# A mixture-of-experts kernel: the last, small groups gathered earlier, and turned inside the first groups of later kinds

## The chip, the cores and the metric

The kernel runs on one core of a Trainium2 chip. The metric is the time of one execution on the device in microseconds (us); several executions are measured and their median is given. The engines are PE (matrix products), DVE (vector), ACT (activation functions), POOL (GpSimd, which here also issues the DMAs with a list of rows) and SP (issues the other DMAs). Each engine runs its own list of instructions in order and waits for the others by semaphores.

## The reference

The input is x of 4 x 1024 tokens of 256 channels. There are two layers, each wrapped as x + layernorm(layer(layernorm(x))). The first is a recurrence over the 1024 steps with a gate; the second is attention with 16 heads followed by four experts, of which each token uses two:

```python
px = einsum('btc,dc->btd', x, W_state) + b_state
g = sigmoid(einsum('btc,dc->btd', x, W_gate) + b_gate)
state = tanh(p_t + state)                  # step by step; out is g_t * state
...
x = x + ao                                 # causal attention, channels 0..63 of ao zeroed
xf = _rms(x, n2_w).reshape(-1, C)
probs = softmax(xf @ gate_w.T)
topv, topi = top_k(probs, 2)               # weights wts, two of four not zero
o0 = gelu(xf @ e0_up.T) @ e0_down.T
o1 = silu(xf @ e1_w1.T) * (xf @ e1_w2.T) @ e1_down.T
o2 = gelu(gelu(gelu(xf @ e2_l1.T) @ e2_l2.T) @ e2_l3.T) @ e2_l4.T
o3 = gelu(gelu(xf @ e3_down.T) @ e3_up.T) @ e3_out.T
moe = wts[:, 0:1]*o0 + wts[:, 1:2]*o1 + wts[:, 2:3]*o2 + wts[:, 3:4]*o3
```

## The kernel before

**Stages.** Up to about 1040 us the kernel computes the recurrence and, beside it, the attention. It writes one row per token into the DRAM tensor `row_d`: 256 channels after attention, 256 of the residual, four expert weights and the factor of the RMS norm (517 numbers). The experts follow, and the change is there.

**Kinds, groups, tails.** The gate sorts the tokens by the pair of experts that they use: six pairs, the *kinds*. Their order of work is `order = [3, 0, 1, 2, 4, 5]`; the place in this order is called the *turn number* n here. So n=0 is the pair (1, 2), n=1 is (0, 1), n=2 (0, 2), n=3 (0, 3), n=4 (1, 3) and n=5 (2, 3). How many tokens a kind has is known only when the kernel runs. A kind is worked off in groups of 256 tokens. Its first group always runs. Each further one stands inside an If (line 1728) on the count and runs if more than 128 tokens are left. What is left then, 1 to 128 tokens, is the kind's *tail*: six Ifs at the very end (line 1742), one for each kind in the same order, each with one group of 128 rows inside. An engine passes each If with a branch of its own; PE gets a hint where its branch will lead. Where an If is not entered, each engine runs a small other block, in which it raises its semaphores to the values that the skipped block would have left. On POOL this includes an instruction that raises the semaphore of a skipped DMA.

**What a group needs.** `fetch` (line 1516) gathers the rows of a group by their numbers, one DMA of 128 rows per half, issued by POOL, into a buffer: `rwfirst` for first groups, `rwsecond` for second ones, `rwnext` for the others, `rwtail` for tails, which have one buffer for each kind. `turn` makes the transposed input: DVE scales the rows (line 1531) into a buffer `x`, PE transposes it into PSUM (line 1538), ACT copies it to SBUF (line 1544). First groups and tails share one buffer `x`, the other groups have another. All turns share one PSUM bank (`tbanks`), which is free again when ACT has copied. `group` runs the products: the layers of the two experts (line 1561 on PE; activations on ACT, line 1622, or for expert 1 a tanh on ACT, line 1629, and DVE, lines 1632 and 1638), the last layer of each (line 1581), and adds their outputs to the rows (line 1649, DVE). Then the layer norm: statistics on DVE (lines 1662 and 1663), z and r on POOL (1669 and 1670), the rest on DVE (1675 and 1678), and a DMA by POOL that writes the rows to `out` (line 1681). Hidden layers pass through three PSUM banks in tails and later groups, two in first groups.

**What sets the order.** A planner written by hand, `plan.run`. Every piece of work is a generator that yields operations with an estimated cost, a priority and the events that it reads; the planner always issues the one that could start first by its own estimate, by priority where several could. What it issues becomes the fixed order of each engine's list. It plans one group at a time: all operations of a call of `group`, those of the list `then` among them, come before the branch that follows.

**Where fetches and turns stand.** A first group of turn n carries in `then`: the gather of its own third group, those of the first and second group of turn n+2, the gather of the tail of turn n−1 (for the last turn also that of its own tail), the turn of the first group of turn n+1, and the turn of its own second group. The first group of n=0 has a list of its own. A tail's turn stands in the tail itself.

Of the kernel before, what the change touches and what calls it, by code (L numbers as in the profile page):

```python
# [31 lines left out]
KINDS = E * (E - 1) // 2  # L32
# [146 lines left out]
class Plan:  # L179
# [14 lines left out]
    def ev(self, *key):  # L194
        return self.events.setdefault(key, Ready())
# [13 lines left out]
    def done(self, *key):  # L209
        self.ev(*key).at = self.end  # L210

    def give(self, *what):

        for w in what:
            if isinstance(w, int):
                self.banks.free[w] = self.end + self.HOP
            else:
                w[0].free[w[1]] = self.end + self.HOP
# [35 lines left out]
def sandwich(  # L254
# [1099 lines left out]
    def gate(pr, w, sm):  # L1354
# [36 lines left out]
    ])  # L1391
    inner.close()
    experts(
        tc, plan, banks, av, ident, mhalf, route, weights, keys, values, row_d, out,
        [after([NT - 1]), experts_input([NI - 1])],
# [4 lines left out]
def experts(  # L1400
# [69 lines left out]
    order = [EARLY] + [c for c in range(KINDS) if c != EARLY]  # L1470
    turn_of = {c: n for n, c in enumerate(order)}

    def kind(n):
        return order[n] if n < KINDS else None


    TAIL = "tail"
    x_tail = slots(KINDS, [P, NCC, P], "xtail").tiles

    def of(c, g):  # L1480
        if g == TAIL:
            return "next", turn_of[c]
        return ("first", turn_of[c] % 2) if g == 0 else ("next", g % 2)

    def xT_of(c, g):
        what, k = of(c, g)
        return x_tail[k] if g == TAIL else xTs[what][k]

    def tiles_of(g):
        return 1 if g == TAIL else NT2  # L1490

    def rows_of(c, g):
        if (c, g) == (EARLY, 0):
            return route["early_rows"]
        n = turn_of[c]
        if g == TAIL:
            return rows["tail"][n]
        what, k = ("first", n) if g == 0 else ("second", n) if g == 1 else ("next", g)
        return rows[what][k % 3]

    def ids_of(c, g, t):
        if (c, g) == (EARLY, 0):
            return route["early"][:, t : t + 1]
        if g == TAIL:
            return route["tails"][:, c : c + 1]
        at = (c * TOKENS + g * N) // P + t
        return ids[:, at : at + 1]

    def fetch(c, g, at=0.0):

        if c is None or g != TAIL and g * N >= TOKENS:
            return
        rw = rows_of(c, g)
        for t in range(tiles_of(g)):
            yield Op("POOL", 1.25, at, [ev("tails" if g == TAIL else "ids")], lag=3.0)
            nc.gpsimd.indirect_dma_start(
                out=rw[:, t, :], out_offset=None, in_=row_d[:, :],
                in_offset=bass.IndirectOffsetOnAxis(ap=ids_of(c, g, t), axis=0),
            )
            done("rows", c, g, t)  # L1520

    def turn(c, g):

        what, k = of(c, g)
        nt = tiles_of(g)
        rw, x = rows_of(c, g), xs["first" if g == TAIL else what][0]
        for t in range(nt):
            got = yield Op("DVE", 0.36, 3.0, [ev("rows", c, g, t)], [] if t else [tbanks["any"]])
            if got:
                tb, = got  # L1530
            nc.vector.tensor_scalar(
                x[:, t, :], rw[:, t, 0:C], rw[:, t, ROW - 1 : ROW], None, ALU.mult
            )
            done("xs", c, g, t)
        yield Op("PE", 0.6, 5.0, [ev("xs", c, g, t) for t in range(nt)], lag=0.2)
        for cc in range(NCC):
            for t in range(nt):
                nc.tensor.transpose(  # L1538
                    tb[0].tiles[tb[1]][:, cc, t * P : (t + 1) * P],
                    x[:, t, cc * P : (cc + 1) * P], ident,  # L1540
                )
        done("xT0", c, g)
        yield Op("ACT", 0.62, 0.5, [ev("xT0", c, g)])
        nc.scalar.copy(xT_of(c, g), tb[0].tiles[tb[1]][:, :, : nt * P])
        give(tb)
        done("xT", c, g)
# [148 lines left out]
    def groups(c, g):  # L1695

        n = turn_of[c]
        more = (g + 1) * N < TOKENS
        label = f"kind{c}group{g + 1}"
        if more and n_of:  # L1700
            hint(label, c, (g + 1) * N + P)
        then = [fetch(c, g + 2)]
        if g == 0:
            then += [fetch(kind(n + 2), 0), fetch(kind(n + 2), 1)]
            for before in [order[n - 1]] if n else []:
                then.append(fetch(before, TAIL, 1.0))
            if n + 1 == KINDS:
                then.append(fetch(c, TAIL, 1.0))
            else:
                then.append(turn(kind(n + 1), 0))  # L1710
        if more:
            then.append(turn(c, g + 1))
        if (c, g) == (EARLY, 0):
            then = [
                *gates, turn(c, 0), fetch(c, 1, 0.0), fetch(kind(1), 0, 1.0), fetch(c, 2, 2.0),
                fetch(kind(1), 1, 3.0), fetch(kind(2), 0, 4.0), fetch(kind(2), 1, 5.0),
                turn(c, 1), turn(kind(1), 0),
            ]
        group(c, g, then)
        if not n_of:  # L1720
            n_of.extend(
                nc.values_load_multi_w_load_instructions(
                    route["counts"][0:1, :], min_val=0, max_val=TOKENS,
                    skip_runtime_bounds_check_because="counts of tokens, only compared",
                )[1]
            )
        if more:
            with tc.If(  # L1728
                n_of[c] > (g + 1) * N + P, preferred_fallthrough_block=True, label=label
            ):  # L1730
                groups(c, g + 1)

    def hint(label, c, at):

        tc.mark_branch_hint_location(label, n_of[c] > at, engines=[mybir.EngineType.PE])

    n_of = []
    for c in order:
        groups(c, 0)
    for n, c in enumerate(order):  # L1740
        hint(f"tail{n}", KINDS + c, 0)
        with tc.If(n_of[KINDS + c] > 0, preferred_fallthrough_block=True, label=f"tail{n}"):
            group(c, TAIL, [turn(c, TAIL)])


# [57 lines left out]
```

## Time and profile before

| | |
|---|---|
| median of 9 runs | 1474.71 us |
| lowest, highest | 1470.46, 1477.03 us |
| the profiled execution | 1471.84 us |
| its span, from first to last instruction | 1470.1 us |
| PE busy | 1311.8 us (89% of the span) |
| DVE, ACT, POOL busy | 896.8, 705.8, 465.6 us |
| mean granted clock of PE | 0.947 of full speed |

The page's row of clocks and its row of PE in 40 slices of the span (36.8 us each, tenths) show where PE is not busy or not at full speed:

```profile
PE   4578787998999998999999999999899999999964
...
PEclk8799899999998989998999999999999999999987
```

Sixteen groups of 256 and two tails run in this execution, by the writes to `out` in the trace: 2 halves of n=0's first group, 10 of the other first groups, 8 of second groups, 12 of later ones, and 2 tails. A wait in the timeline stands in brackets after the instruction that waited: how long its engine was idle before it, and what ended that. A small q after an engine (POOLq) means its queue of instructions: branches, semaphores and the issuing of DMAs, which are not counted as busy. DMA issues by POOL are shown with the time that it takes to issue them, not with that of the transfer.

### The profile page before, as it was taken

The page shows a single profiled execution, that of the slowest core. Times are in us where ns is not written, and L with a number is a line of the kernel's source. Part 1 is how long each engine was busy: PE and PEld are TensorE (multiplying, and loading weights), DVE is VectorE, ACT ScalarE, POOL GpSimd, SP SyncE. Part 2 cuts the span into 40 slices and gives each one's busy share as a digit, 9 for nine tenths or more (in the row PEclk, how much of TensorE's full clock was granted, in tenths as well). Part 3 has the DMA queues.
Part 4 walks back from the last instruction along what each step waited for, and adds up shares of the span by engine and source line. Part 5 has one row for each costly group of instructions (what it writes and reads, how often), then busy time and mean ns, then how long its engine had stood idle before and what let it go on. Part 6 is the DMA issues. An engine that isn't in the chain of part 4 may idle for free. (4 is left out here: it accounts for less than half of the span.)

```text
span 1470.1 us, 43267 instructions
## 1 busy us (share of the span) xinstructions
PE 1311.8 (89%) x17455; PEld 1020.8 (69%) x17470; DVE 896.8 (61%) x2738; ACT 705.8 (48%) x2144; POOL 465.6 (32%) x1466
## 2 busy tenths in 40 slices
PE   4578787998999998999999999999899999999964
PEld 2235456666676776687677677878688889888764
DVE  5566578599688778778877987784614312113311
ACT  2345555655765765776665455657222222223211
POOL 2433534535444444334311101101223322214221
PEclk8799899999998989998999999999999999999987
DMA  4010010001010000001000100121222220103110
GB/s 127 22 51 2 2 44 16 17 2 46 3 31 17 3 21 29 3 4 45 3 4 9 40 3 4 41 102 62 61 78 66 57 61 26 40 23 83 52 46 5
DMA packets 35917, 49.57 MB, mean 34 GB/s; under 512 B 7638, under 2 KB 27862, under 8 KB 35670
## 3 DMA queue, kind: packets, MB, share of 16 engines
q1 hardware_dynamic: 28774, 25.20, 5.6%
q0 software_dynamic: 6624, 20.62, 5.0%
q8 instruction: 147, 2.41, 0.7%
q14 instruction: 100, 0.82, 0.2%
q10 hardware_dynamic: 272, 0.52, 0.1%
HBM read 32.87 MB, written 13.46 MB: 32 GB/s over the span
## 5 line engine op out<-in xcount | busy, mean ns | idle before, releaser
L1024 ACT ACTIVATE ex<-bank 128x512 f32<-128x512 f32 (+1 forms) x592 | 326.0, 582 | 153.1 <-PE bank L883 87.6
L883 PE MATMUL bank<-keys,q 32*128 32x128 f32 x4608 | 352.6, 293 | 16.4 <-ACT q L762 3.6
L583 POOL TENSOR_TENSOR s<-keys 128x8 f32<-128x8 f32 x1023 | 223.3, 218 | 384.6 <-ACT keys L586 373.7
L883 PE MATMUL bank<-q,keys 32*128 32x128 f32 x4608 | 334.5, 293 | 7.0 <-ACT ex L1024 4.5
L883 PEld LDWEIGHTS bank<-q,keys 32*128 32x128 f32 x4608 | 273.3, 192 | 77.5 <-issue 41.6
L586 ACT ACTIVATE keys<-s 128x8 f32<-128x8 f32 x1023 | 218.5, 214 | 211.7 <-POOL s L583 209.1
L883 PEld LDWEIGHTS bank<-keys,q 32*128 32x128 f32 x4608 | 293.0, 193 | 36.2 <-DVE nm L975 6.3
L975 DVE TENSOR_REDUCE nm<-bank 128x1 f32<-128x512 f32 (+4 forms) x336 | 203.1, 639 | 52.6 <-PE bank L883 44.2
L968 DVE CUSTOM_DVE_ANT_0 bank<-bank,late 128x512 f32<-128x512 f32 (+2 forms) x320 | 188.4, 622 | 50.3 <-PE bank L883 49.1
L1044 POOL TENSOR_SCALAR_AFFINE_SELECT ex<-ex 128x256 f32<-128x256 f32 (+1 forms) x240 | 102.7, 429 | 262.0 <-ACT ex L1024 261.1
L1065 PE MATMUL av<-ex,values 128*17 128x128 f32 x4608 | 175.2, 282 | 2.9 <-DVE avT L1084 1.1
L1561 PE MATMUL bank<-values,keys 128*128 128x256 f32 x568 | 134.4, 383 | 5.9 <-PEq L1728 2.3
L1065 PEld LDWEIGHTS av<-ex,values 128*17 128x17 f32 x4608 | 110.0, 99 | 40.2 <-issue 16.1
L1561 PEld LDWEIGHTS bank<-values,keys 128*128 128x128 f32 x568 | 106.4, 191 | 22.0 <-issue 3.5
L1622 ACT ACTIVATE keys<-bank 128x256 f32<-128x256 f32 (+1 forms) x136 | 50.4, 371 | 147.7 <-PE bank L1561 147.6
L1561 PE MATMUL bank<-keys 128*128 128x256 f32 x384 | 84.8, 379 | 0.0
L1561 PEld LDWEIGHTS bank<-keys 128*128 128x128 f32 x384 | 73.0, 190 | 9.9
L534 PE MATMUL bank<-big,wsg 128*128 128x512 f32 x128 | 63.9, 644 | 5.9 <-ACT big L472 5.9
L711 PE MATMUL bank<-wqk,big 128*128 128x512 f32 x128 | 65.2, 638 | 3.2 <-ACT big L472 3.2
L1622 ACT ACTIVATE hid<-bank 128x256 f32<-128x256 f32 x66 | 25.3, 383 | 86.5 <-PE bank L1561 86.5
L1649 DVE SCALAR_TENSOR_TENSOR rwnext<-av,rwnext 128x192 f32<-128x192 f32 x24 | 8.9, 414 | 93.4 <-PE av L1581 93.4
L1669 POOL TENSOR_SCALAR z<-mv 128x2 f32<-128x2 f32 (+1 forms) x18 | 4.1, 227 | 187.1 <-DVE mv L1663 165.7
(265 smaller groups left out, 1785.4 us busy)
## 6 DMA issues: line engine op xcount, KB each, us to landing
row_d<-xn SPq DMA_DIRECT2D x16, 512.0 KB
xn<-in_x SPq DMA_DIRECT2D x8, 512.0 KB
xc<-in_x SPq DMA_DIRECT2D x7, 512.0 KB
keys<-in_e_l SPq DMA_DIRECT2D x2, 1024.0 KB
keys<-in_e_w SPq DMA_DIRECT2D x2, 512.0 KB
keys<-in_e_down SPq DMA_DIRECT2D x2, 384.0 KB
xc<-in_x SPq DMA_DIRECT2D x4, 128.0 KB
wsg<-in_w_sg ACTq DMA_DIRECT2D x1, 512.0 KB
```

The lines of the kernel that those rows point to most:

```text
L534: nc.tensor.matmul(pb, lhsT=wsg[:, cc, half * C + dc * P : half * C + (dc + 1) * P], rhs=lnT[:, cc, :], start=(cc == 0), stop=(cc == NCC - 1),
L583: nc.gpsimd.tensor_tensor(s, st[:, :, t], prev, ALU.add)
L586: nc.scalar.activation(st[:, :, t], s, AF.Tanh)
L711: nc.tensor.matmul(pqk, lhsT=hT[:, cc, b * P : (b + 1) * P], rhs=wqk[:, cc, :], start=(cc == 0), stop=(cc == NCC - 1),)
L883: nc.tensor.matmul(banks.tiles[pbs[j]][:, m * P : (m + 1) * P], lhsT=k if kind == "sT" else q, rhs=q if kind == "sT" else k, start=(m == 0 ...
L968: nc.vector.tensor_tensor_reduce(out=s_, in0=s_, in1=late[:, 4 * P - w :], scale=-1.0, scalar=FMAX, op0=ALU.add, op1=ALU.min, accum_out=by ...
L975: nc.vector.tensor_reduce(by_slot[:, half, h0:h1, 2 * p + j], banks.tiles[pb][:, m0 * P : m1 * P].rearrange("p (h w) -> p h w", h=h1 - h0) ...
L1024: nc.scalar.activation(exs.tiles[ex[1]][:, j, : step.w], banks.tiles[pb][:, : step.w], AF.Exp)
L1044: nc.gpsimd.affine_select(out=d, in_=d, pattern=pattern, compare_op=ALU.is_ge, fill=0.0, base=0, channel_multiplier=-1,)
L1065: nc.tensor.matmul(av[32 * j : 32 * j + HD + 1, hc, :], lhsT=v_all[:, b, kb, 4 * hc + j, :], rhs=exs.tiles[ex[j // 2][1]][:, j % 2, m * P ...
L1561: nc.tensor.matmul(hb[0].tiles[hb[1]][:, :w_], lhsT=w[:, j, m * P : (m + 1) * P], rhs=src[:, j, :w_], start=(j == 0), stop=(j == nk - 1),)
L1622: nc.scalar.activation(to, src, AF.Gelu)
```

## The change

The gathers of tails move to earlier first groups: n=1 now issues those of n=0, 1 and 2, and n=2, 3 and 4 that of n+1; n=5 issues none. The turns of tails move out of the tails: the first group of n=2 turns the tails of n=0 and 1, that of n=3 the tail of n=2, that of n=4 the tail of n=3, and that of n=5 the tails of n=4 and 5. Gathers and turns are then made for all six tails, also for those that have no tokens; before, all six were gathered, and only the tails that run were turned. The tails' groups start from the turned input.

```diff
         then = [fetch(c, g + 2)]
         if g == 0:
             then += [fetch(kind(n + 2), 0), fetch(kind(n + 2), 1)]
-            for before in [order[n - 1]] if n else []:
-                then.append(fetch(before, TAIL, 1.0))
-            if n + 1 == KINDS:
-                then.append(fetch(c, TAIL, 1.0))
-            else:
+
+            if n:
+                got = range(3) if n == 1 else (n + 1,)
+                turned = {2: (0, 1), KINDS - 1: (KINDS - 2, KINDS - 1)}.get(n, (n - 1,) if n > 1 else ())
+                then += [fetch(kind(k), TAIL, 1.0) for k in got]
+                then += [turn(kind(k), TAIL) for k in turned]
+            if n + 1 < KINDS:
                 then.append(turn(kind(n + 1), 0))
         if more:
             then.append(turn(c, g + 1))
...
         with tc.If(n_of[KINDS + c] > 0, preferred_fallthrough_block=True, label=f"tail{n}"):
-            group(c, TAIL, [turn(c, TAIL)])
+            group(c, TAIL, [])
```

## The prediction

> **What bounds the kernel now.** I read the chain of waits first: its last 100 us go through the tails (the last groups, of at most 128 tokens). Two of six are computed: the timeline shows two writes from rwtail, and their products tell the kinds, turns n=3 (experts 0 and 3) and n=4 (experts 1 and 3).
>
> ```profile
> 1404.24 37.22 DMA rwnext<-row_d,ids
> 1441.46 0.07 POOLq L1742
> ...
> 1441.79 0.23 POOL z L1669
> ```
>
> A gather does not take 37 us (others land in 3.3 to 5.0 us). The queue's own instructions at the tails' If, L1742, tell what POOL did in that time:
>
> ```profile
> L1742 POOLq COMPARE_BRANCH  x8: 38/42/50, 1434.5 to 1458.9; - x8
> ...
> L1742 POOLq INC_SWDGE_SEM  x4: 2041/2052/2080, 1434.8 to 1459.2; - x4
> ```
>
> Each tail that is not there costs POOL a semaphore increment of 2.05 us: it comes to the tails at 1434.5, skips n=0, 1, 2 at about 2.3 us each, and is at tail n=3 at 1441.46. The timeline around it:
>
> ```profile
> 1423.65 1.06 POOL L1681 DMA_INDIRECT out<-rwfirst,ids  x1 [1.20 <-DVE rwfirst L1678]
> ...
> 1428.73 0.99 POOL L1681 DMA_INDIRECT out<-rwfirst,ids  x1 [4.02 <-DMA out<-rwfirst,ids]
> 1429.70 0.35 DVE L1531 TENSOR_SCALAR values<-rwtail 128x256 f32<-128x256 f32 x1 [5.56 <-DVEq L1742]
> ...
> 1441.06 0.18 DVE L1663 BATCH_NORM_AGGREGATE mv<-st 128x2 f32<-128x6 f32 x1
> 1441.79 0.23 POOL L1669 TENSOR_SCALAR z<-mv 128x1 f32<-128x1 f32 x1 [12.07 <-DMA rwnext<-row_d,ids]
> ...
> 1443.57 0.35 DVE L1531 TENSOR_SCALAR values<-rwtail 128x256 f32<-128x256 f32 x1
> ...
> 1448.22 0.29 DVE L1632 SCALAR_TENSOR_TENSOR tnext<-tnext,bank 128x128 f32<-128x128 f32 x1 [4.30 <-ACT tnext L1629]
> ...
> 1455.56 0.42 DVE L1649 SCALAR_TENSOR_TENSOR rwtail<-av,rwtail 128x192 f32<-128x192 f32 x1 [0.76 <-PE av L1581]
> ```
>
> Tail 3's statistics are ready at 1441.24, POOL at 1441.46: a dead heat. A turn that leaves tail 3 gains nothing, since POOL's path to 1441.46 does not contain it. Before all that, PE is the bound: from 1112 to 1419 the timeline shows it nearly gapless. What matters there is the end of a first group, here turn n=2:
>
> ```profile
> 1186.85 0.60 PE L1538 MATMUL bank<-ident,values 128*128 128x128 f32 x4
> ...
> 1187.48 0.58 ACT L1544 COPY values<-bank 128x512 f32<-128x512 f32 x1 [2.45 <-PE bank L1538]
> ...
> 1188.12 4.58 PE L1561 MATMUL bank<-values,keys 128*128 128x256 f32 x20 [0.68 <-ACT values L1544]
> ```
>
> The last transposes, 0.63 to the copy, 0.58 for it, and only then the next group's first product: its xT comes from the last turn.
>
> **The change part by part.** *Gathers moved.* Six before and after; n=1 issues three for one, n=5 none for two. One costs 0.95 + 0.30 (gap) = 1.25 us of POOL. In n=5 POOL then idled 12.39 us before its next work: nothing gained, nor by landing sooner, since the tail's first DVE step waited for DVEq (its branches), not for a DMA. In n=1 nothing covers it:
>
> ```profile
> 1130.12 0.95 POOL L1516 DMA_INDIRECT rwtail<-row_d,tails  x1 [0.30 <-issue]
> 1131.10 0.23 POOL L1669 TENSOR_SCALAR z<-mv 128x2 f32<-128x2 f32 x1
> ...
> 1134.52 6.21 PE L1561 MATMUL bank<-values,keys 128*128 128x256 f32 x28
> ```
>
> So z moves by 2.50. Behind it on DVE wait L1675/L1678, then the next group's L1531, L1632 (1134.01 to 1134.42) and L1638 (1135.59 to 1136.01), which free PE's banks. PE's 28 products are seven sets of 0.887. Two run freely, to 1136.30; the third waits for L1632, now 1136.92 (0.66 lost), and ends at 1137.85; the fourth waits for L1638, now 1138.51 (0.70 lost). The rest follow. **+1.36**; bounds 0.7 (one wait only) and 2.5 (all of it).
>
> *Turns added.* A tail's two transposes take 0.22 in PE's stream (four take 0.43: 1183.81 to 1184.24). All turns share one PSUM bank, so each waits for the copy of the one before, and the order of the changed kernel puts them thus:
>
> n=2: tail 0 sits where the next kind's turn sat (0.21 saved); tail 1, the next kind's and this kind's second group come after the last product, where one turn stood before. With d = 1186.84 as DVE's first L1649: L1649s, L1662, L1663 until d+1.36 as now, then L1531 of the next kind, d+1.28 to d+1.89 = 1188.73; its last transposes until 1189.35; copy to 1189.93. DVE now has the second L1662/L1663, then the last L1531, to 1189.85. Transposes 1190.0 to 1190.6, copy to 1191.21, first product 1191.27 for 1188.12: **+3.15**. Bounds 2.0 (DVE's pair free at once, one copy round of 1.25 after the other) and 3.9.
>
> n=3: tail 2 takes the gap, two turns follow the last product. The same steps from d = 1335.17: L1531 ends 1337.06, copy 1337.65 to 1338.23, first product 1338.29 for 1336.51: **+1.78** (1.2 to 2.4).
>
> n=4: all three lie between products, tail 3 adds 0.22; DVE's L1632/L1638 come in time by the same reckoning. **+0.22** (0 to 0.6). n=5: two tails' 0.44 replace 0.43 before the last product, and the displaced turn follows it, for a group that does not run: **0** (0 to 0.3). ACT's four more copies of 0.37 stand in its idle time (the page's ACT rows idle for PE).
>
> All this moves L1649 of n=5, and with it POOL's writes, increments and tail 3, one for one: 1.36 + 3.15 + 1.78 + 0.22 = **+6.51**.
>
> *Tail 3:* POOL binds, **0**. *Tail 4:* DVE leaves tail 3 at 1443.59 as now, but the x is turned, and PE has run tail 4 as far as the bank that L1632 frees. So L1632 comes at 1443.6 for 1448.22: −4.6. The 7.34 us from there to the last L1649 are PE's at full clock. Clock is the catch:
>
> ```profile
> 1371.00:1372.00 1.00, 0.39 (x2) 0.00 (x0) 0.00 (x0) 0.38 (x1) 0.00 (x0) 1.00 0.36 131
> 1372.00:1373.00 1.00, 0.00 (x0) 0.00 (x0) 0.03 (x1) 0.00 (x0) 0.00 (x0) 0.90 0.00 0
> 1373.00:1374.00 1.00, 0.55 (x1) 0.50 (x2) 0.92 (x3) 0.00 (x0) 0.88 (x1) 0.50 0.02 8
> ```
>
> (us; busy PE, PEld, DVE, ACT, POOL; granted clock; DMA.) After a wait of 2.06 us with little work before it, the clock was 0.50 until 1379.7. Its changes in this trace (1372.9, 1379.7, 1424.0, 1434.1, 1444.5, 1447.95) lie multiples of about 3.4 us apart; the intervals before the drops were under 45% busy. PE's own branches end near 1429 (its last compare at L1742 starts at 1428.6); tail 3 takes it 8.7 (1431.33 to 1440.04 now), its share of tail 4, 20 products and a branch, about 3: near 1441 it is done and waits some 3 us for DVE. I take one interval at half clock, 1.7 lost: **−2.9** (−4.6 without it, −1.2 with two).
>
> *Clock inside.* At the end of n=2 PE idles 1.5 + 0.7 + 0.7 of 4.2 us, at n=3 1.4 + 0.65 of 3.3. Depending on where the intervals fall, about 70% and 50% of positions leave one under 45% busy. I take one interval in all, **+1.7** (0 to 5.1).
>
> The Trainium skill, "TensorE: Matmul & The Clock Gate", section "HAM oscillation — how this bites in real kernels", asks only that no idle gap exceed about 3.4 us. By that rule no place here would drop, and the sum would be +6.5 − 4.6 = +1.9; the row at 1373, a drop after 2.06 us, speaks against it.
>
> **Sum:** 6.51 + 1.7 + 0 − 2.9 = **+5.3 us**. On the profiled execution (1471.84, of it 1470.1 span) that is 1477.1. That execution lies 2.87 below the median of 1474.71, to which I add the difference: **1480.0 us**. About 0.2% (2.95 us) can be told from no change here.
>
> **The rivals.** (a) *Clock stays up everywhere:* +6.5 − 4.6 = +1.9, 1476.6, no change that can be told. For it: idles of 1.9 and 1.45 us near 1048 and 1052 left the clock at 1.00. Against: the row above. 25%.
> (b) *Clock falls at both ends of groups, and stays down for two intervals in the tail:* 6.5 + 5.1 − 1.2 = +10.4, 1485.1. For it: the drop at 1372.9 lasted two intervals. 12%.
> (c) *Faster: the added turns hide.* If they end before the next group's product is due at n=2 and n=3, only the six pairs of transposes stay (1.3) with n=1's 1.36, and tail 4 gives 4.6; POOL also could use a quicker landing of the last write (2.24 us of idle as in other groups, for 4.02: 1.8), which L1531 at 1429.70 masked until now. 1.3 + 1.36 − 4.6 − 1.8 = −3.7, 1471.0. Decides: whether PE's gap at 1188 stays below 1 us. Against: the last turn feeds the very next product, through one bank. 8%.
>
> **How the numbers follow.** Forecast 55%, mostly beyond +2.95; (a) 25%, a fifth of it too. Slower 0.67, same 0.25, faster 0.08. Bounds all low: 3.9 + 0 − 4.6 = −0.7; all high: 9.7 + 5.1 − 1.2 = +13.6. Leaving out a tenth at each end: 1475.5 to 1485.
>
> **What would show it.** In the changed profile: PE's first product after n=2's first group waits for ACT's copy, after three bursts of transposes, about 3 us later against the last product; half of that at n=3; z of n=1 2.5 us later against the third rwfirst gather; DVE's last L1649 less than 8 us after tail 3's L1678 (now 12.4); POOL still four increments of 2.05. Wrong if the tails' z follows mv, not POOL's increments, or if PE has no gap over 1 us at those ends.

## The result, and the profile after

| | before | after |
|---|---|---|
| median, us | 1472.2 (39 runs, 1468.8 to 1482.11) | 1476.93 (12 runs, 1474.2 to 1479.02) |
| ratio after / before | | 1.0022, 95% interval 1.0010 to 1.0034 |
| profiled execution, us (its span) | 1471.84 (1470.1) | 1476.58 (1474.9) |

The change makes the kernel slower by about 3.2 us (1.5 to 5.0). That is the ratio's figure: the means of these runs are 1473.20 and 1476.41 us, while the medians lie 4.7 apart. The forecast was +5.3, with 1480.0 us and a range of 1475.5 to 1485, counted from the nine runs of the kernel before that were known then (median 1474.71). Line numbers from 1702 on are two higher in the changed kernel: its Ifs of the groups are L1730, those of the tails L1744.

**The end of n=2's first group.** The timeline (start, duration, engine, line, operation; in brackets the idle time before it and what ended it):

```profile
1188.74 0.38 PE L1538 MATMUL bank<-ident,values 128*128 128x128 f32 x2
...
1190.72 0.72 PE L1538 MATMUL bank<-ident,values 128*128 128x128 f32 x4 [1.60 <-DVE values L1531]
...
1192.12 0.85 PE L1538 MATMUL bank<-ident,values 128*128 128x128 f32 x4 [0.68 <-ACT values L1544]
...
1193.65 1.65 PE L1561 MATMUL bank<-values,keys 128*128 128x256 f32 x3 [0.68 <-ACT values L1544]
```

Three bursts stand after the last product, as the forecast said, and the next group's product starts 4.71 us after DVE's L1649 (1188.94) where it took 1.07 before. But its first three matmuls take 1.65 us; six take 1.56 at full clock in a profile shown further down. The busy time by stretches shows why (us; busy PE, PEld, DVE, ACT, POOL; granted clock; DMA):

```profile
1191.00:1192.00 1.00, 0.44 (x4) 0.20 (x3) 0.85 (x4) 0.52 (x1) 0.37 (x1) 1.00 0.00 0
1192.00:1193.00 1.00, 0.85 (x4) 0.46 (x4) 0.23 (x1) 0.06 (x1) 0.72 (x1) 0.72 0.00 0
1193.00:1194.00 1.00, 0.35 (x1) 0.35 (x2) 0.93 (x3) 0.59 (x1) 0.07 (x1) 0.50 0.00 0
...
1198.00:1199.00 1.00, 1.00 (x4) 0.75 (x3) 0.00 (x0) 0.00 (x0) 0.70 (x2) 0.50 0.25 90
1199.00:1200.00 1.00, 1.00 (x6) 0.87 (x5) 0.00 (x0) 0.38 (x1) 0.70 (x2) 0.87 0.12 41
```

The clock is at half for two intervals; busy PE time by the missing share of the clock, summed over these stretches, gives 3.0 us.

**n=1.** Three gathers of tails stand ahead of z:

```profile
1130.99 0.94 POOL L1516 DMA_INDIRECT rwtail<-row_d,tails  x1 [0.30 <-DVE mv L1663]
...
1132.24 0.94 POOL L1516 DMA_INDIRECT rwtail<-row_d,tails  x1 [0.30 <-issue]
...
1133.49 0.94 POOL L1516 DMA_INDIRECT rwtail<-row_d,tails  x1 [0.30 <-issue]
1134.45 0.24 POOL L1669 TENSOR_SCALAR z<-mv 128x2 f32<-128x2 f32 x1
...
1137.85 2.38 PE L1561 MATMUL bank<-values,keys 128*128 128x256 f32 x8 [0.51 <-DVE tnext L1632]
```

z comes at 1134.45 for 1131.10; 0.92 of the 3.35 us were there before the experts' first changed group, so 2.43 are the two gathers. PE waits for L1632, as forecast.

**The tails:**

```profile
1436.81 0.99 POOL L1681 DMA_INDIRECT out<-rwfirst,ids  x1 [3.25 <-DMA out<-rwfirst,ids]
...
1440.34 2.90 PE L1561 MATMUL bank<-xtail,keys 128*128 128x128 f32 x12 [11.73 <-PEq L1744]
...
1450.91 0.18 DVE L1663 BATCH_NORM_AGGREGATE mv<-st 128x2 f32<-128x6 f32 x1
...
1451.26 0.23 POOL L1669 TENSOR_SCALAR z<-mv 128x1 f32<-128x1 f32 x1 [13.46 <-DVE mv L1663]
...
1452.63 0.42 DVE L1678 TENSOR_TENSOR rwtail<-rwtail 128x256 f32<-128x256 f32 x1
1452.98 0.28 DVE L1632 SCALAR_TENSOR_TENSOR tnext<-tnext,bank 128x128 f32<-128x128 f32 x1
...
1460.30 0.42 DVE L1649 SCALAR_TENSOR_TENSOR rwtail<-av,rwtail 128x192 f32<-128x192 f32 x1 [0.76 <-PE av L1581]
...
1461.63 0.23 POOL L1669 TENSOR_SCALAR z<-mv 128x1 f32<-128x1 f32 x1 [7.21 <-DVE mv L1663]
```

Two things differ from what was forecast. Tail 3's z now waits for mv: before, POOL was ready 12.73 us after it began its last write (1428.73 to 1441.46); by the same time it is ready at 1449.54, and mv ends at 1451.09. PE is late in spite of the turn that it no longer has to do there. Its queue shows a part of it; the first line is before's stretch 1418 to 1422, the second the changed kernel's 1425 to 1432 (count, shortest/median/longest in ns, first and last start):

```profile
L1742 PEldq COMPARE_BRANCH  x2: 1442/2205/2968, 1419.7 to 1421.5; - x2
```

```profile
L1744 PEldq COMPARE_BRANCH  x1: 3128/3128/3128, 1429.4 to 1429.4; - x1
```

The first of three branches took 3.13 us for 1.44. So the first product comes 10.07 us after n=5's last z, where it came after 9.91 with the turn ahead of it; and the clock, at half after the branches, stays so for 4.7 us of tail 3's products, where it was 2.9. And in tail 4 L1632 comes 0.35 us after L1678 (5.06 before), the last L1649 7.32 after that, and no half clock is in it.

**Where the time went.** The table takes the same instructions from the timelines of all 18 profiles. The columns are the parts of the way that they bound (L1649s come in pairs, one for each half; the first of a pair counts): n=1 (DVE's first L1649 of its first group to the last pair of its second), n=2 (on to the first L1649 of its second group, so with the end of its first), n=3 (the same there), "to n=4" (on to the first L1649 of n=4; its start holds before's 3.1 us at half clock), n=4/5 (to n=5's last L1649), z5-z3 (n=5's last z to tail 3's) and z3-z4 (to tail 4's). Row one is in us, the others are differences to it:

```
                          n=1    n=2    n=3  to n=4  n=4/5  z5-z3  z3-z4
before                  25.22  67.07 135.44  35.66   37.38  20.37  15.10
after                   +1.16  +6.21  +1.84  -1.61   +0.33  +0.62  -4.73
before_again            +0.83  +0.02  -0.01  -1.51   +0.01  +0.96  +0.95
after_again             +3.16  +3.24  +2.55  -3.33   +0.34  +0.29  -4.73
after_third             +4.98  +3.25  +2.02  -3.33   +0.34  +0.15  -4.72
gathers_alone           +1.18   0.00  +0.07  -3.33    0.00  +1.03  +0.99
n2_turns_alone          +1.19  +6.27  -0.01  -3.05    0.00  +1.15  +0.23
n2_turns_again          +4.63  +3.25  -0.01  -1.67    0.00  +1.72  +0.22
n3_turn_alone           +1.13  +0.07  +3.49  -3.36   +0.01  +1.04  +1.02
last3_alone              0.00  +0.07  +0.06  -3.33   +0.28  -1.20  +1.10
last4_alone             +0.67  +0.01  +0.12  -3.34   +0.22  +0.41  -4.73
last34_alone            +0.01   0.00   0.00  -3.36    0.00  -0.13  -4.73
spread_at_ends          +0.67  +3.56  +1.97  -1.74   +0.33  +0.73  -4.73
turns_early             +1.09  +1.72  +1.98  -3.11   +1.86  +0.51  -4.73
turns_in_stream         +1.28  +0.44  +0.22  -1.40   +0.44  -1.78  -4.73
in_stream_again         +3.37  +0.45  +0.21  -1.45   +0.45  -0.32  -4.73
spread_in_stream         0.00  +0.23  +0.21  -3.13   +0.66  -0.60  -4.73
spread_in_stream_again  +0.73  +0.30  +1.15  -3.07   +0.66  -2.10  -4.73
```

The row "after" with the 0.92 from before n=1 makes 0.92 + 1.16 + 6.21 + 1.84 - 1.61 + 0.33 + 0.62 - 4.73 = 4.74: the spans differ by 4.8. The table also says how far one profile can be trusted: row one itself is the odd one out in two places. The 3.1 us at half clock on the way to n=4 are in none of the others in full, and in eleven of 17 they are missing altogether (-3.05 to -3.36); z5-z3 and z3-z4 are shorter there than in any other kernel that turns the tails in their places.

### The profile page after: what moved, and what is told of

It is laid out like the page before. It is cut to its first block, busy times and chain, and to the rows that moved or that the text cites. A ratio compares the mean times of both kernels' runs of the same rounds, so it can differ in the third digit from the quotient of the medians.

```text
span 1474.9 us, 43293 instructions
## 1 busy us (share of the span) xinstructions
PE 1315.1 (89%) x17463; PEld 1022.3 (69%) x17478; DVE 897.7 (61%) x2742; ACT 707.3 (48%) x2148; POOL 465.8 (32%) x1466
## 5 line engine op out<-in xcount | busy, mean ns | idle before, releaser
L1649 DVE SCALAR_TENSOR_TENSOR rwnext<-av,rwnext 128x192 f32<-128x192 f32 x24 | 8.9, 413 | 93.4 <-PE av L1581 93.4
```

## The experiments

The runs were made on four chips, each with runs of the kernel before beside them; a ratio is always to those. gathers_alone, the first runs of n=2's and n=3's turns and turns_early shared a chip (before 1473.36 us), so did last34_alone, last3_alone, turns_in_stream and spread_in_stream (1472.43), then the two unaltered kernels, last4_alone and spread_at_ends (1481.89), and the last four (1483.1).

### The gathers alone

```diff
-                turned = {2: (0, 1), KINDS - 1: (KINDS - 2, KINDS - 1)}.get(n, (n - 1,) if n > 1 else ())
+                turned = ()
...
-            group(c, TAIL, [])
+            group(c, TAIL, [turn(c, TAIL)])
```

> Only the gathers stand as in the changed kernel (three tails in n=1, none in n=5); all turns stay in the tails. By the forecast's terms: z of n=1 comes 2.5 us later against the third rwfirst gather, and the time is +1.36 us (0.7 to 2.5) against before, ratio 1.0009; the tails cost what they did (last z of n=5 to the end of the span within 0.5 us of before). Rival, the gathers hide or are paid back by an emptier POOL in n=5: +0.3 us or less, ratio 1.0002 or below. The profile of the changed kernel (transposes after n=1's last product 2.09 us later, 0.92 of that from before the change) speaks for +1.2.

Ratio 1.0003 (0.9986 to 1.0020). That is too wide to tell 1.4 us from nothing. The profile tells more: n=1 is 1.18 longer and no other part pays it back, so the term of +1.36 holds on this chip. On the chips of the last eight runs the kernels with one gather in n=1 are already 0.67 to 0.83 longer there than the first profile, and those with three 3.16 to 4.98: the two gathers cost 2.4 to 4.3 there, 1.5 to 1.7 of it at half clock in two of the four. The timeline of n2_turns_again shows PE waiting inside n=1 for ACT, and ACT's own wait put down to "remote":

```profile
1145.90 0.38 ACT L1622 ACTIVATE keys<-bank 128x256 f32<-128x256 f32 x1 [2.47 <-remote]
...
1146.33 3.37 PE L1581 MATMUL av<-keys 128*128 128x192 f32 x10 [2.26 <-ACT keys L1622]
```

What ACT waits for there was not found out.

### Two turns in n=2 alone, twice; one turn in n=3 alone

```diff
-                turned = {2: (0, 1), KINDS - 1: (KINDS - 2, KINDS - 1)}.get(n, (n - 1,) if n > 1 else ())
+                turned = (0, 1) if n == 2 else ()
...
-            group(c, TAIL, [])
+            group(c, TAIL, [] if n in (0, 1) else [turn(c, TAIL)])
```

For n=3 the same with `(2,) if n == 3` and `(2,)`.

> As the run with the gathers alone, and the turns of tails 0 and 1 stand in n=2 (neither tail exists with these data, so the tails that run are as before). By the forecast's terms: +1.36 +3.15 = +4.5 us against before, ratio 1.0031, with PE's first product after n=2's first group 3.2 us later against the last product of that group. The changed kernel's profile shows half clock there from 1192.7 to 1199.1, about 3 us more: if that comes with the bursts each time, +7.5 us, ratio 1.0051. Rival, the time lost at n=2 is made good behind it (a later interval at half clock falls away, as at n=4's start in the changed kernel): +1.4 to +2.5, ratio 1.0010 to 1.0017.

> The gathers as in the changed kernel and the turns of tails 0 and 1 in n=2, all others in the tails, a second time. If the clock falls at n=2's end by rule: 6.2 us lost there again. If by chance: 3.2, as in the second profile of the changed kernel. The time: +4.4 to +7.5 against before, ratio 1.0030 to 1.0051 (1.0043 measured).

> As the run with the gathers alone, and the turn of tail 2 stands in n=3. By the forecast's terms: +1.36 +1.78 = +3.1 us against before, ratio 1.0021, with PE's first product after n=3's first group 1.8 to 2.1 us later against the group's last L1649, and no drop of the clock there. Rival, a drop of the clock comes with the one burst too: +4.8 us, ratio 1.0033. Rival, hidden: as the gathers alone.

n=2: ratios 1.0043 (1.0028 to 1.0058) and 1.0069 (1.0045 to 1.0093). In the profiles n=2 costs 6.27 in the first, with two intervals at half clock (3.0), and 3.25 in the second, without. n=3: 1.0024 (1.0009 to 1.0040); its part costs 3.49, with one interval at half clock (1.7); the changed kernel, without one, has 1.84. So the bursts cost what the forecast took, 3.15 and 1.78, and the clock comes on top in some executions. The rival that the loss is made good behind it falls: against gathers_alone the columns from n=3 to z5-z3 are shorter by 0.1 at most, and only z3-z4 is, by 0.8. The second ratio is above what was expected; its profile has 4.63 in n=1.

### The tails' gain alone

```diff
-            else:
+            then += [turn(kind(k), TAIL) for k in ((3, 4) if n == KINDS - 1 else ())]
+            if n + 1 < KINDS:
                 then.append(turn(kind(n + 1), 0))
...
-            group(c, TAIL, [turn(c, TAIL)])
+            group(c, TAIL, [] if n in (3, 4) else [turn(c, TAIL)])
```

This is the kernel before with the two tails that exist turned in n=5; the other two runs move tail 3 or tail 4 alone.

> The kernel before, with the turns of tails 3 and 4 alone moved into n=5 (gathers as before, all other turns in the tails). It shows the gain in the tails by itself. By the forecast: n=5 0 to 0.3, tail 3 0 (POOL's increments bind), tail 4 -2.9 (-4.6 and one interval of half clock): ratio 0.9980. By the changed kernel's trace: no fall of the clock in tail 4, -4.7, but tail 3's statistics come up to 1.4 after POOL is ready, since PE's own branches take longer: -3.3 to -4.7, ratio 0.9968 to 0.9978, and 7.7 us from tail 3's L1678 to the last L1649. Rival, the clock takes the gain back: 0 to -1.2, ratio 0.9992 to 1.0000.

> The kernel before, with the turn of tail 3 alone moved into n=5. By the forecast's term (POOL binds at tail 3): 0, ratio 1.0000, tail 3's z right after POOL's third increment. Rival, PE binds: the turn's 2.3 us between PE's branches and its first product are saved, and the statistics come sooner, but z waits for POOL all the same: still 0, with mv 1 to 2 us ahead of z. Rival, from the changed kernel's trace (first branch of PE 3.13 us for 1.44, its first product 11.7 us after its last work as before): mv is no sooner, and z waits for mv, 0 to +1.5, ratio up to 1.0010.

> The kernel before, with the turn of tail 4 alone moved into n=5. By the forecast's term: -2.9 us, ratio 0.9980. By the runs: 10.37 us between the two tails' z for 15.1 to 16.2 (mean 15.8 of five kernels that turn tail 4 in its place), -5.4 us, ratio 0.9963, and no half clock in tail 4. Tail 3 as before: z 21 us after n=5's last z, released by mv in most executions.

Tail 4 alone 0.9963 (0.9951 to 0.9975), 5.5 us; both 0.9961 (0.9946 to 0.9975), 5.7 us; tail 3 alone 0.9991 (0.9979 to 1.0002), 1.3 us and not told from nothing. The term for tail 4 was -2.9: too small by half. The two z's of last4_alone in its timeline:

```profile
1453.63 0.23 POOL L1669 TENSOR_SCALAR z<-mv 128x1 f32<-128x1 f32 x1 [12.18 <-DVE mv L1663]
...
1464.00 0.23 POOL L1669 TENSOR_SCALAR z<-mv 128x1 f32<-128x1 f32 x1 [7.21 <-DVE mv L1663]
```

10.37 us, and so (to 0.01) in all eleven profiles that turn tail 4 early: no interval at half clock in any. And the same stretch in gathers_alone, where the turn is in its place:

```profile
1445.17 0.23 POOL L1669 TENSOR_SCALAR z<-mv 128x1 f32<-128x1 f32 x1 [13.17 <-DVE mv L1663]
...
1447.46 0.66 PE L1538 MATMUL bank<-ident,values 128*128 128x128 f32 x2 [3.66 <-DVE values L1531]
...
1448.15 0.37 ACT L1544 COPY xtail<-bank 128x256 f32<-128x256 f32 x1 [5.34 <-PE bank L1538]
...
1448.58 2.93 PE L1561 MATMUL bank<-xtail,keys 128*128 128x128 f32 x12 [0.46 <-ACT xtail L1544]
...
1461.26 0.23 POOL L1669 TENSOR_SCALAR z<-mv 128x1 f32<-128x1 f32 x1 [12.93 <-DVE mv L1663]
```

Here PE waits 3.66 us for DVE with nothing to do, and then runs twelve products in 2.93, at half clock (1.50 for the first twelve of tail 4 in the changed kernel, at full clock). z to z is 16.09. The seven profiles with tail 4's turn in its place have 15.10 to 16.20, mean 15.74: turning it early takes away 5.4, the wait and the half clock that it brings. Half clock costs the seven 1.5 to 2.7 us, and without it each takes 13.5 to 13.6: so some 3.2 of the 5.4 are the wait, 2.2 the clock.

Tail 3's z5-z3 is 21.27 in the mean of the seven profiles with its turn in its place and 20.02 in the eleven without: 1.25. But they come from several chips. On the one that has two of each (before_again and last4_alone, after_again and spread_at_ends) the means are 21.06 and 20.88, and the time of tail 3 alone is not told from nothing either: that its turn costs about a microsecond there is not shown. In six of those seven, z comes 0.4 to 2.5 us after POOL could be ready (12.73 after its last write's start); only the profile that the forecast was read from has POOL last.

### The same turns at other places in PE's list

turns_early gives the transposes of tails the first place among what PE could do next; turns_in_stream also takes DVE's step for 3 us longer, in the plan alone; spread_in_stream also spreads gathers and turns; spread_at_ends has the gathers of the kernel before and one turn to a group (three in n=5), at PE's old last place.

```diff
-            got = yield Op("DVE", 0.36, 3.0, [ev("rows", c, g, t)], [] if t else [tbanks["any"]])
+            got = yield Op("DVE", 0.36, 3.0, [ev("rows", c, g, t)], [] if t else [tbanks["any"]], lag=3.0 if g == TAIL else 0.0)
...
-        yield Op("PE", 0.6, 5.0, [ev("xs", c, g, t) for t in range(nt)], lag=0.2)
+        yield Op("PE", 0.6, 0.5 if g == TAIL else 5.0, [ev("xs", c, g, t) for t in range(nt)], lag=0.2)
...
-                got = range(3) if n == 1 else (n + 1,)
-                turned = {2: (0, 1), KINDS - 1: (KINDS - 2, KINDS - 1)}.get(n, (n - 1,) if n > 1 else ())
+                got = {1: (0,), 2: (1,), 3: (2, 3), 4: (4, 5)}.get(n, ())
+                turned = {2: (0,), 3: (1,), 4: (2,), 5: (3, 4, 5)}.get(n, ())
```

The second change alone is turns_early, the first two are turns_in_stream, all are spread_in_stream.

> The changed kernel with the same gathers and the same turns in the same groups, but the tails' transposes take the first place among PE's ready work instead of the last, so that they stand between products and the ends of n=2 and n=3 are as in the kernel before. If the serial bursts at the group ends are the cost: no gap of PE over 1 us there, no drop of the clock at n=2; 1.36 for the gathers, six pairs at 0.22 = 1.3, and tail 4's gain of 4.7, less up to 1.5 for PE's branches at tail 3: -2.0 to -0.5 us against before, ratio 0.9987 to 0.9997, some 4 to 5 us below the changed kernel. Rival, the added turns cost by their number or by DVE and ACT, not by where they stand: like the changed kernel, ratio 1.0022. Rival, the gain of tail 4 is taken back by the clock: 0 to +1.5, ratio 1.0000 to 1.0010.

turns_early: 0.9994 (0.9982 to 1.0006), as the first theory expected. The interval reaches into the second rival's range too, but z3-z4 keeps its whole gain of 4.73, so the clock did not take it back. The ends of n=2 and n=3 are as before, but the parts still cost 1.72 and 1.98. Its timeline at n=2:

```profile
1168.07 0.35 DVE L1531 TENSOR_SCALAR values<-rwtail 128x256 f32<-128x256 f32 x1 [2.88 <-DVEq L1730]
...
1168.48 0.44 PE L1538 MATMUL bank<-ident,values 128*128 128x128 f32 x2 [1.05 <-DVE values L1531]
```

DVE is idle for 2.88 us at its branch out of the groups before, which the plan does not know; PE, in order, stops at the transposes and waits. Hence the next runs.

> As the run with the turns early, but the plan takes DVE's step of a tail's turn for 3 us longer, so that the transposes stand three or more products later, after DVE has really come out of its branch. If PE's waits for DVE's L1531 (1.05 at n=2, 1.55 at n=3, 1.20 at n=5 in that run) were what its turns cost: these waits go, n=2 and n=3 cost 0.2 to 0.5 each, and the time is 1.16 (gathers in n=1) + 1.3 - 4.7 + up to 1.4 at tail 3 = -2.2 to -0.8 us against before and some 3 us less than that run inside, ratio 0.9985 to 0.9995. Rival, the turns cost by number: as that run or worse. Rival, gathers in n=1 cost nothing: ratio 0.9977.

> As turns_in_stream (the changed kernel's gathers and turns, transposes between products), a second time: n=1 +1.2, n=2 to n=5 0.2 to 0.5 each, tails -5.4 and -1.0: -4 us, ratio 0.9973; 0.9966 measured.

> As the run before it in this list, but n=1 gathers one tail again (n=2 one, n=3 and n=4 two each) and the turns stand one each in n=2, n=3, n=4 and three in n=5. If the gathers in n=1 are worth what the profiles show (1.1 to 1.2), the time is that run's less 1.2: -3.4 to -2.0 us against before, ratio 0.9977 to 0.9986, with n=1's last L1649 to the transposes of the next group as before. Rival, the gathers are hidden: like that run.

> As spread_in_stream, a second time: n=1 0, n=2 to n=5 0.2 to 0.7 each, tails -5.4 and -1.0: -5.1 us, ratio 0.9965; 0.9973 measured. It should lie 1.2 us below the run before it in this list if the two gathers in n=1 are the only difference that tells.

turns_in_stream, n=2:

```profile
1168.82 0.35 DVE L1531 TENSOR_SCALAR values<-rwtail 128x256 f32<-128x256 f32 x1 [2.70 <-DVEq L1730]
...
1171.65 0.38 PE L1538 MATMUL bank<-ident,values 128*128 128x128 f32 x2
```

No wait is left, and n=2 and n=3 cost 0.44 and 0.22: 0.22 for each pair of transposes, the price that the forecast took from four in 0.43. The ratio is 0.9966 (0.9955 to 0.9977) on one chip and 0.9999 (0.9984 to 1.0014) on another, where the three gathers in n=1 cost 2.6 more than one. spread_in_stream, with one gather there, has 0.9973 (0.9957 to 0.9990) and 0.9970 (0.9954 to 0.9985) on the same two: 4.0 and 4.4 us under the kernel before. It does the work of the changed kernel, is faster than the kernel before on both chips, and faster than the changed kernel on the one where both ran (1477.95 and 1485.85). That it would lie 1.2 below turns_in_stream did not show on the first chip; on the second the difference was 4.2.

> The turns of tails 0, 1, 2 stand one each in n=2, n=3, n=4 and those of 3, 4, 5 in n=5; the gathers are as in the kernel before (one in n=1 to n=4, two in n=5), and the transposes keep the last place among PE's work, so that one burst more stands at the ends of n=2 and of n=3. By the forecast's terms: 1.78 for n=2, 1.78 for n=3, 0.22, and -2.9 in the tails: +0.9, ratio 1.0006. By the runs: 1.84 at each end, 3.5 where the clock falls, 0.3, and -5.4 -1.2 in the tails: -2.6 without a fall, -0.9 with one, +0.7 with both, ratio 0.9982 to 1.0005. Rival, the clock falls at n=2's end for two intervals even with one burst: +2, ratio 1.0014.

spread_at_ends: 1.0017 (1.0002 to 1.0031), above all that was summed for it but the rival's figure. In its profile n=2 has one interval at half clock even with one burst more (3.56, of it 1.7), n=3 1.97. What else its executions pay is not seen in that one profile.

### Both kernels again, unaltered

> The kernel before, unaltered: ratio 1.0000, and its interval is the yardstick for the others. The prediction read the 3.1 us of half clock at the start of n=4 (1372 to 1380) and the 15.10 us from tail 3's z to tail 4's z as properties of the kernel. If they are, a second profile shows both within 0.5 us. The other runs speak against it: kernels that are the same as this one there show no half clock at n=4 (gathers alone, n=2's turns alone, n=3's turn alone, tail 3's turn alone) and 15.3 to 16.2 us from z to z. Then this profile has 0 to 1.7 us lost at n=4 and about 15.8 from z to z.

> The changed kernel, unaltered, beside the others of this list: ratio 1.0022 as measured, +1.5 to +5 us. If the fall of the clock at n=2's end follows from its two added bursts, it is there again (3.0 us lost near 1192 to 1200), and 10.37 us lie between the two tails' z, with no fall of the clock in tail 4. If it was chance, n=2 costs 3.2 to 3.6 and not 6.2.

> The changed kernel, unaltered, a third time. By the sum of what the runs showed: 1.2 (n=1), 3.2 at n=2 and 0 to 3.0 for the clock there (2.0 taken), 1.8 to 2.5 at n=3, 0.3 at n=4, -5.4 in tail 4 and -1.0 at tail 3: +2.1 to +3.0 without the first bound's spread, ratio 1.0014 to 1.0021. By the mean of the two measured ratios: 1.0028. By the prediction: +5.3, ratio 1.0036.

before_again: 0.9997 (0.9983 to 1.0011). Its profile has 1.51 less on the way to n=4 and 15.10 + 0.95 from z to z: neither figure of the first profile is a constant of the kernel. The changed kernel: 1.0050 (1.0028 to 1.0072) and 1.0028 (1.0009 to 1.0048), beside the 1.0022 first measured. The end of n=2 in after_again:

```profile
1203.95 0.72 PE L1538 MATMUL bank<-ident,values 128*128 128x128 f32 x4 [1.60 <-DVE values L1531]
...
1205.34 0.66 PE L1538 MATMUL bank<-ident,values 128*128 128x128 f32 x4 [0.68 <-ACT values L1544]
...
1206.67 1.56 PE L1561 MATMUL bank<-values,keys 128*128 128x256 f32 x6 [0.68 <-ACT values L1544]
```

```profile
1205.00:1206.00 1.00, 0.66 (x4) 0.42 (x4) 0.12 (x2) 0.29 (x1) 0.88 (x2) 1.00 0.00 0
1206.00:1207.00 1.00, 0.33 (x2) 0.30 (x3) 0.97 (x3) 0.59 (x1) 0.00 (x0) 1.00 0.00 0
```

The same gaps to the hundredth as in the changed kernel's first profile, and the clock stays at 1.00: n=2 costs 3.24, where 3.15 was forecast. So the fall does not follow from the two bursts alone: it is there in two of the five profiles that have them. What it depends on can be read from the traces. In each of the 18 profiles the changes of the granted clock lie whole multiples of 3.41 us apart, as the forecast had read from one. The end of n=2 divided at these times (columns as above), first the changed kernel's first profile, then after_again:

```profile
1189.03:1192.44 3.41, 1.13 (x8) 0.78 (x8) 2.72 (x10) 0.96 (x2) 0.80 (x2) 1.00 0.00 0
```

```profile
1201.35:1204.77 3.42, 1.71 (x11) 1.18 (x9) 2.47 (x10) 0.44 (x2) 0.00 (x0) 1.00 0.00 0
1204.77:1208.18 3.41, 2.16 (x11) 1.77 (x12) 2.46 (x8) 1.44 (x3) 2.12 (x3) 1.00 0.00 0
```

In the first, one interval holds the gaps of 1.60 and 0.68 us whole: PE is busy for 1.13 of its 3.41 us (33%), and the next two intervals are at half clock. In the second these two gaps fall into two intervals, 50% and 63% busy, and the clock stays. The others agree: n2_turns_alone has an interval of 33% and a fall, after_third and n2_turns_again have none under 51% and no fall. At n=3's end n3_turn_alone has 40% and a fall, the changed kernel's three profiles have 57% or more and none; spread_at_ends has 45% at n=2's end and a fall. From 1060 us on, in all 18 profiles, every interval at full clock that was less than 46% busy was followed by one at half clock, and no other was (between 1000 and 1060 us five that were 47 to 56% busy were so too). So the gaps are the kernel's; where the intervals lie over them differs from one execution to the next. The 1.0050 is not explained by its profile: summed over the table, after_again is 0.3 us over before_again, the spans differ by 2.4 and the medians by about 7. Where the rest lies stays open.

## Why the prediction was wrong in size, point by point

**Gathers in n=1, +1.36:** right on the first two chips, too small on the others. 1.16 in the changed kernel, 1.09 to 1.28 in the five other profiles with three gathers on the first two chips; 2.4 to 4.3 on the other two, for which the wait for ACT in n2_turns_again is a sign, not an explanation.

**Turns, +3.15 at n=2, +1.78 at n=3, +0.22 at n=4, 0 at n=5:** right. Without a fall of the clock 3.24 and 3.25; 1.84, 2.02 and 2.55 (the last just over the bound of 2.4); 0.33 for n=4 and n=5 together. The sum inside was 6.51; 1.16 + 3.25 + 1.84 + 0.33 is 6.6. The three bursts, the order of the waits (DVE's L1531, ACT's copy, ACT's copy) and the gap of more than 1 us are there as written.

**Clock inside, +1.7:** right as a mean. The clock fell at n=2's end in two of the five profiles with two bursts more, for 3.0 us each, and at n=3's end in one of the five with one burst more, for 1.7: 1.2 + 0.3, about 1.6 in the mean. The mechanism held as well: intervals of 3.41 us, a fall behind one that is less than 45% busy. Only the shares of positions were taken high: moved over the rows of after_again, the intervals leave one under 45% in an estimated 56% of positions at n=2's end and 30% at n=3's, for 70% and 50%. The Trainium skill, "TensorE: Matmul & The Clock Gate", section "HAM oscillation — how this bites in real kernels", would have no fall here, since no gap reaches 3.4 us; the row at 1193 with 0.50 after gaps of 1.60 and 0.68 differs from it, the rows of after_again agree.

**Tail 4, -2.9: this step failed.** It read "near 1441 it is done and waits some 3 us for DVE. I take one interval at half clock, 1.7 lost". The wait is never 3 us: it is 1.12 to 1.19 us in ten of the eleven profiles with the early turn and 1.92 in the one where POOL releases tail 3's z (spread_in_stream). The forecast let PE leave its branches near 1429, 7.6 us after n=5's last z, and DVE leave tail 3 at POOL's time. In the changed kernel the branches end 9.9 us after that z, tail 3's z follows PE's work, and PE reaches the wait only at 1452.13, while DVE's L1632, for which it waits, ends at 1453.26. Behind so short a wait no interval at half clock follows: no interval over it is under 50% busy, and all eleven have 10.37 us from z to z. The kernels with the turn in its place wait 3.65 to 4.03 us there; each of the seven has an interval of 12 to 30% behind which the clock falls, and loses 1.5 to 2.7 us. So the gain is 4.73 against the profile that the forecast was read from, close to its bound of -4.6 without a loss, and 5.4 against the mean (15.74), since that profile lost only 1.5 to half clock.

**Tail 3, 0: half right.** That POOL is last at tail 3 was this one execution's, where the two came within 0.22 us (1441.24 and 1441.46). In the other six of the seven profiles with the turn in its place the statistics come last, so the path does contain the turn, and in the changed kernel z behind mv met the forecast's own mark for being wrong. What taking the turn away saves stays open: 1.25 by the means over all chips (20.02 for 21.27), 0.2 on the one chip with two of each. In the changed kernel a longer first branch (3.13 for 1.44) and more half clock take its place.

**Sum:** 6.6 + 1.6 - 5.4 - 1.25 = +1.6 by what the runs showed, for a forecast of 6.51 + 1.7 + 0 - 2.9 = +5.3; measured +3.2 (1.5 to 5.0). Without tail 3's 1.25, which is not shown, it is +2.8. The direction and the parts inside held, the gain in the tails was taken at 2.9 and is 5.7 by last34_alone. By that, rival (a), "clock stays up everywhere", had nearly the right tail but left out the clock inside, and its sum of +1.9 lay within the interval. Rival (c) was refuted where the turns stand at the ends, and comes true for the plan in which they are hidden: spread_in_stream reaches -4.0 and -4.4 for its -3.7, but by another sum (no gathers added in n=1, 5.4 in tail 4), so that the nearness of the figures is luck.

## What to carry to other kernels

Work that is moved off a tail costs by where it lands in the in-order list of the bound engine: at the end of a group, behind one PSUM bank, two small turns cost 3.2 us, between products 0.22 each. A plan that puts it between products must know when its producer really arrives, the 2.9 us of DVE's branch included. Before a stretch at half clock or a dead heat is read from one profile as a property of the kernel, look for it in a second execution. Whether gaps of PE bring half clock was decided here by how they lie to intervals of 3.41 us: the gaps of 1.60 and 0.68 us cost only themselves where they fell into two, and 3.0 us more where they fell into one.

## What the hardware showed that was not expected

The same gaps of PE (1.60, 0.68, 0.68 us) were followed by two intervals at half clock or by none, as one interval of 3.41 us held the first two of them whole (33% busy) or not (50% and more). In an earlier stage, from 1033 to 1059 us, untouched by any of these kernels, the loss to half clock was 2.7 to 2.8 us in ten profiles, 6.3 to 6.6 in four and 8.1 to 8.2 in four; that alone moves an execution by some 4 us or more, more than the whole change. And PE's branch past a tail that is not there is no constant: the first took 1.44 us in one profile and 3.13 in the other, the next ones 2.97 to 3.27, while the shortest of all eight took 0.08. Over the 18 profiles the first takes 1.1 to 3.3 us; it is short in both profiles of the kernel before and long in all three of the changed one, and why was not found out. The Trainium skill, "Advanced Engine Details and Errata", section "Control Flow Timing", gives about 108 ns for a compare-and-branch; these rows differ from it by up to thirty times.
